# Routing of a mixture of experts in fewer VectorE steps, mixing weights made among the expert blocks, and blocks in another order

## The chip, the cores and the metric

The kernel runs on one core of a Trainium2 chip. Five engines work side by side, each through its own queue in order: TensorE (PE; its weight loads are listed as PEld), VectorE (DVE), ScalarE (ACT), GpSimd (POOL) and SyncE (SP), which issues most transfers. The metric is the device time of one execution in microseconds. A profile of one execution gives the start and the duration of every instruction.

## The reference

A small vision tower: a tokenizer, then layer 0 (attention across images, then six experts of which each row takes two), then layer 1 (a linear attention, then shared and gated MLPs). All is in float32. The part that the change touches is the end of layer 0's attention and its mixture:

```python
h = h + attention(layernorm(h))
x = layernorm(h)
rh = relu(x @ router_w1 + router_b1)
p = softmax(rh @ router_w2 + router_b2)          # 6 experts
top_w, top_i = top_k(p, 2)
weight = softmax(top_w)
out_e = (relu(relu(x @ w1[e] + b1[e]) @ w2[e] + b2[e])) @ w3[e] + b3[e]
h = h + sum of weight * out_e over the two experts chosen
```

There are four images of 784 rows. A row's six logits decide where its normalised row is sent, and its two weights are used only when the experts' results are fetched again for layer 1.

## The kernel before, in words

**Layout.** Rows of an image stand in six tiles of 128 rows with a rest of 16; the four rests share one more tile. A *unit* of routing is what is routed in one go: image 0 (six tiles), image 1 (six), image 2 (six), the first four tiles of image 3, and its last two with the tile of rests (three). So there are five units.

**Attention rounds** (`added_rows` and `weighed`, called for images 1 and 2, and a written-out round for image 3). The order of DVE, PE, ACT and SP is written by hand there. A round for image s does three things in turn on the same engines: the attention of image s (`products`: one DVE pass over 784 columns for each other image, whose sums go to PE as the matmul `pl`; `values`: four more passes a half), the output product of image s-1 with its residual (`attended`), and the routing of image s-2 (`choose`, `count`, `send`).

- `attended` multiplies by `Wo` on PE and adds to `h` on DVE (L965), which also leaves the row sum in `nm`. A tensor_scalar (L969) turns the sums of two or three tiles into minus the mean. ACT then squares `h` minus the mean with a sum (L973).
- `scales_of` takes the root on ACT (L982), `shifts_of` the reciprocal and the product with the mean on DVE (L987, L988). ACT (and for one unit DVE) writes the normalised rows.
- `roots_next` is a dummy Sqrt on one number (`spot`, L922) that makes ACT fetch the Sqrt table before the root needs it.
- `router_logits` makes the logits of a unit on PE in the one buffer of `psum_s`. `choose` (L1058 to L1092) adds the bias on DVE, finds the best and the second expert of every row, and makes running counts of rows per expert over the unit's tiles, starting from `running`. `count` sums the ranks below each row on PE. `send` adds the experts' base addresses `base0` on DVE (L1118), picks each row's place, casts it into `pos` (L1126), and POOL sends the rows to DRAM by indirect DMA (L1129), two for each tile.
- `mix1`, `mix2`, `mix3` turn the two best logits into the two weights `wk`: Exp on ACT, sum, reciprocal and a product on DVE, Exp on ACT, then three DVE steps.

**Where the mixing stands.** For image 0 it is in `weighed(2)`, for image 1 in the written-out round, and for the last three units together behind block 5 of the experts.

**Blocks.** After routing, the rows of an expert lie together in DRAM. They are worked on in 30 blocks: 24 full ones of 256 rows and six small ones of 128, for what is left over. The first seven (`NEARLY`) are full blocks that images 0 and 1 alone fill. They run while the later units are still routed, in a written-out stretch. For block i: SP loads the rows (`load`), PE transposes them (`turned`, `ptb`), ACT copies them out as `xTb`, DVE copies the expert's weights to `own` at an offset which it first loads into a register (`own_weights`, L1487, 1540 columns), PE makes two hidden layers (`hidden`, `pb`, L1511) whose relu goes to ACT (half o = 0) and to DVE or ACT (half o = 1), and `rows_back` makes `pyb` on PE (L1529), adds a bias on DVE (`yb`, L1535) and stores the result through SP.

From block 7 on one loop writes the order: for each i, `load(i + 3)`, `hidden(i, 0)`, `rows_back(i - 1)`, `own_weights(i + 1)`, `turned(i + 1)`, `hidden(i, 1)`. In this loop only DVE, SP and POOL keep the order as written; a scheduler places ACT's and PE's instructions. `order` lists which block comes when: seven early, three full, six small, fourteen full. `after` says behind which block the rows of the first units of layer 1 may be fetched.

Of the kernel before, what the change touches and what calls it, by code (L numbers as in the profile page):

```python
# [29 lines left out]
NI = 4  # L30
# [42 lines left out]
def tile_vit_tower(ctx: ExitStack, tc: tile.TileContext, a: dict, out: bass.AP):  # L73
# [107 lines left out]
    nc.gpsimd.memset(nothing, 0.0)  # L181
    base0 = const.tile([TT, E0], F32, tag="base0", name="base0")
# [768 lines left out]
    def attended(s, two, block=None):  # L951

        if s not in sums:
            sums[s] = [
                small.tile([TT, TPI + 1], F32, tag=tag, name=tag) for tag in ("nm7", "ss7", "r7")
            ]
        nm, ss, r = sums[s]
        pm = mm_rows(
            two, lambda c, j: (
                oL[:, c].rearrange("p b n -> p (b n)") if j == TPI else oTs[s][:, c, cut(j, 1)]  # L960
            ), Wo, "pwo"
        )
        for i, j in enumerate(two):
            ht = h[:, s * TPI + j, :]
            nc.vector.scalar_tensor_tensor(  # L965
                ht, pm[:, i, :], 1.0, ht, ALU.mult, ALU.add, accum_out=nm[:, j : j + 1]
            )
        part = nm[:, two[0] : two[-1] + 1]
        nc.vector.tensor_scalar(part, part, -1.0 / D, None, ALU.mult)  # L969
        if block is not None:  # L970
            turned(block)
        for j in two:
            nc.scalar.activation(  # L973
                junk, h[:, s * TPI + j, :], AF.Square, bias=nm[:, j : j + 1],
                accum_out=ss[:, j : j + 1],
            )


    def scales_of(u):
        b, j0, n = u  # L980
        nm, ss, r = (x[:, j0 : j0 + n] for x in sums[b])
        nc.scalar.activation(r, ss, AF.Sqrt, scale=1.0 / D, bias=eps[:TT])  # L982

    def shifts_of(u):
        b, j0, n = u
        nm, ss, r = (x[:, j0 : j0 + n] for x in sums[b])
        nc.vector.reciprocal(r, r)  # L987
        nc.vector.tensor_tensor(nm, nm, r, ALU.mult)  # L988
# [44 lines left out]
    def router_logits(u):  # L1033
        b, j0, n = u
        rT = turned0.pop(u)
        pr = psum_s.tile([P, 512], F32, tag="pss", name="plg")
        for j in range(n):
            nc.tensor.matmul(
                pr[:TT, j * E0 : (j + 1) * E0], rT[:, cut(j, 1)], rw2, start=True, stop=True
            )  # L1040
        logits0[u] = pr[:TT, : n * E0].rearrange("p (j e) -> p j e", e=E0)
# [3 lines left out]
    def choose(u):  # L1045
# [6 lines left out]

        def wide(x):
            return x.unsqueeze(2).to_broadcast([TT, n, E0])

        rk = rank[E0][:TT].unsqueeze(1).to_broadcast([TT, n, E0])
        lg = t7("lg7", n, E0)
        nc.vector.tensor_tensor(lg, logits0.pop(u), over(rb2, n), ALU.add)  # L1058
        m = t7("m7", n)
        nc.vector.tensor_reduce(m, lg, AX.X, ALU.max)  # L1060
        nc.vector.tensor_tensor(lg, lg, wide(m), ALU.subtract)
# [6 lines left out]
        second = t7("second7", n)  # L1068
# [7 lines left out]
        tiles = t7("tiles7", n + 1, E0)  # L1076
        if running[0] is None:
            nc.vector.memset(tiles[:, 0, :], 0.0)
        else:
            nc.vector.tensor_copy(tiles[:, 0, :], running[0])  # L1080
        nc.vector.tensor_tensor(tiles[:, 1:, :], sel[:, 0], sel[:, 1], ALU.add)
        if n == 6:
            odd = tiles[:, :6].rearrange("p (k i) e -> p k i e", i=2)
            nc.vector.tensor_tensor(odd[:, :, 1], odd[:, :, 1], odd[:, :, 0], ALU.add)
            nc.vector.tensor_tensor(
                tiles[:, 2:4], tiles[:, 2:4], over(tiles[:, 1], 2), ALU.add
            )
            nc.vector.tensor_tensor(tiles[:, 6], tiles[:, 6], tiles[:, 5], ALU.add)
            nc.vector.tensor_tensor(tiles[:, 4:], tiles[:, 4:], over(tiles[:, 3], 3), ALU.add)
        else:  # L1090
            for j in range(n):
                nc.vector.tensor_tensor(tiles[:, j + 1], tiles[:, j + 1], tiles[:, j], ALU.add)  # L1092
        running[0] = tiles[:, n, :]
# [3 lines left out]
    def count(u):  # L1097
# [6 lines left out]
        for k in range(2):  # L1104
# [4 lines left out]
            out_, allones[:TT, :TT], tiles[:, :n, :].rearrange("p j e -> p (j e)"), start=False, stop=True  # L1109
        )  # L1110
        picked[u] = sel, out_.rearrange("p (j e) -> p j e", e=E0)

    def send(u):
# [3 lines left out]
        at = small.tile([TT, n, E0], F32, tag="at7", name="at7")  # L1117
        nc.vector.tensor_tensor(at, before_, over(base0, n), ALU.add)  # L1118
        nc.vector.tensor_tensor(
            sel, sel, at.unsqueeze(1).to_broadcast([TT, 2, n, E0]), ALU.mult  # L1120
# [264 lines left out]
    def weighed(s):  # L1385
# [26 lines left out]
        if s > 1:  # L1412
            mix1(past)
            mix2(past)
# [5 lines left out]
        if s > 1:  # L1420
            mix3(past)
# [28 lines left out]
    order += [(2, i) for i in range(NSMALL)]  # L1450
    order += [(1, i) for i in range(FIRST, NFULL - NEARLY)]
# [124 lines left out]
    with tc.manual_schedule(engines=by_hand | {ENG.SP}):  # L1576
# [3 lines left out]
        mix1(past)  # L1580
# [7 lines left out]
        mix2(past)  # L1588
# [7 lines left out]
        mix3(past)  # L1596
# [73 lines left out]
        for v in (u, ua, ub):  # L1670
            mix1(v)
        hidden(6, 1)
        for v in (u, ua, ub):
            mix2(v)
        for v in (u, ua, ub):
            mix3(v)
# [146 lines left out]
    for u, (b, j0, n) in enumerate(units[:2]):  # L1823
        last = (b * TPI + j0 + n) * TT
        most = {2: 8, 3: 13}[-(-last // BLK)]
        after[u] = order.index((1, most - 1))
    after[LU] = after[2] = NBLK - 1
    assert after[0] < after[1] < NBLK - 1
    with tc.manual_schedule(engines={ENG.DVE, ENG.SP, ENG.Pool}):
        own_weights(NEARLY)  # L1830
        turned(NEARLY)
        for i in range(NEARLY, NBLK + 1):
# [8 lines left out]
            if i == NEARLY + 1:  # L1841
                centred_weights()
            for u in (0, 1, LU, 2):
# [587 lines left out]
```

## Time and profile before

| what | us |
|---|---|
| median of three executions | 735.71 (733.22 to 735.82) |
| the profiled execution's own time | 733.79 |
| its span | 732.1 |
| tokenizer and keys, up to the first round | 0 to about 181 |
| rounds of images 1 and 2 | 181 to 240 |
| last round and wait for the first block | 240 to 263 |
| first seven blocks with routing | 263 to 318 |
| blocks 7 to 29 | 318 to 437 |
| layer 1 | 437 to 732 |

A timeline row has the start, the busy time, engine, line and operation, what is written from what, shapes and a count; in brackets stands how long the engine had been idle before it and who ended that. A row of waits has who waited for whom, then the total, the number of times and the longest. A row by stage has start and end, the length, busy time of PE, PEld, DVE, ACT and POOL (instructions in brackets), the granted TensorE clock, the share of the DMA engines and GB/s.

### The profile page before, as it was taken

The page shows a single profiled execution, that of the slowest core. Times are in us where ns is not written, and L with a number is a line of the kernel's source. Part 1 is how long each engine was busy: PE and PEld are TensorE (multiplying, and loading weights), DVE is VectorE, ACT ScalarE, POOL GpSimd, SP SyncE. Part 2 cuts the span into 40 slices and gives each one's busy share as a digit, 9 for nine tenths or more (in the row PEclk, how much of TensorE's full clock was granted, in tenths as well). Part 3 has the DMA queues.
Part 4 walks back from the last instruction along what each step waited for, and adds up shares of the span by engine and source line. Part 5 has one row for each costly group of instructions (what it writes and reads, how often), then busy time and mean ns, then how long its engine had stood idle before and what let it go on. Part 6 is the DMA issues. An engine that isn't in the chain of part 4 may idle for free.

```text
span 732.1 us, 9866 instructions
## 1 busy us (share of the span) xinstructions
PE 684.2 (93%) x3023; PEld 471.4 (64%) x3023; DVE 480.6 (66%) x1486; ACT 322.7 (44%) x787; POOL 125.0 (17%) x232
## 2 busy tenths in 40 slices
PE   7889988999998879997899998999999999999996
PEld 4636655656566568786788884677776855555553
DVE  5689886778999765455444766779968654354441
ACT  1545546555865663432222326655545232222231
POOL 5400000000034717600003035762000000000000
PEclk9999999999999899999999999999999999999999
DMA  6899999000014754422324352331000014321333
GB/s 181 282 423 418 420 417 414 5 1 1 0 56 138 258 176 157 154 93 67 100 87 130 100 165 76 92 85 40 1 1 1 4 30 119 118 92 54 115 99 102
DMA packets 56477, 96.49 MB, mean 132 GB/s; under 512 B 6697, under 2 KB 46351, under 8 KB 56425
## 3 DMA queue, kind: packets, MB, share of 16 engines
q1 hardware_dynamic: 49924, 79.69, 31.0%
q0 software_dynamic: 5600, 14.32, 6.5%
q10 hardware_dynamic: 900, 1.86, 0.8%
q8 instruction: 24, 0.39, 0.2%
q14 instruction: 29, 0.23, 0.1%
HBM read 30.75 MB, written 65.09 MB: 131 GB/s over the span
## 4 chain that ended last, share of the span: by engine, by line
PE 54%; DVE 6%; ACT 2%; issue 1%; DMA 1%; DVEq 1%; SPq 0%; ACTq 0%
PE pb L1511 12%; PE pe L315 6%; PE pyb L1529 5%; PE ps L315 5%; PE pqk L1972 4%; PE ps L2381 3%; PE pout L2151 3%; PE pout L2156 3%; PE pukx L2071 2%; PE pt L306 2%; PE pe L2351 2%; PE ps L2375 2%; PE ptb L1496 1%; DVE own L1487 1%; PE pkvo L2131 1%
## 5 line engine op out<-in xcount | busy, mean ns | idle before, releaser
L1129 POOL DMA_INDIRECT xrows<-xn,pos x50 | 53.1, 1063 | 220.3 <-DVE nm L988 179.5
L1729 POOL DMA_INDIRECT ys<-yrows,pos x50 | 48.8, 976 | 138.3 <-DMA yrows<-yb 120.6
L1511 PE MATMUL pb<-xTb,own 128*128 128x256 f32 (+1 forms) x240 | 54.4, 371 | 9.3 <-DVE own L1487 8.2
L1517 ACT ACTIVATE hb<-pb,own 128x256 f32<-128x256 f32 (+1 forms) x74 | 33.8, 457 | 56.0 <-PE pb L1511 49.7
L1511 PEld LDWEIGHTS pb<-xTb,own 128*128 128x128 f32 x240 | 41.7, 195 | 17.5 <-ACT hb L1517 6.4
L1511 PE MATMUL pb<-hb,own 128*128 128x256 f32 (+1 forms) x240 | 52.2, 360 | 0.5 <-DVE hb L1519 0.5
L1529 PE MATMUL pyb<-own,hb 128*128 128x256 f32 x216 | 51.8, 381 | 0.2 <-ACT hb L1517 0.2
L315 PE MATMUL pe<-xT,eW 128*128 128x512 f32 (+1 forms) x112 | 46.0, 553 | 0.0
L1972 PE MATMUL pqk<-Wqkv,lxT 128*128 128x512 f32 x100 | 44.9, 594 | 0.2 <-ACT lxT L94 0.2
L1529 PEld LDWEIGHTS pyb<-own,hb 128*128 128x128 f32 x216 | 40.3, 190 | 5.9 <-ACT hb L1517 0.6
L1511 PEld LDWEIGHTS pb<-hb,own 128*128 128x128 f32 x240 | 40.4, 190 | 4.9 <-DVE hb L1519 1.2
L630 PE MATMUL pw<-Wall,pT 128*128 128x512 f32 (+1 forms) x96 | 42.5, 593 | 0.0
L1500 ACT COPY xTb<-ptb 128x512 f32<-128x512 f32 (+1 forms) x30 | 16.3, 543 | 57.7 <-PE ptb L1496 57.7
L1535 DVE TENSOR_TENSOR yb<-pyb,eb 128x512 f32<-128x512 f32 (+1 forms) x30 | 19.1, 638 | 33.9 <-PE pyb L1529 33.5
L1519 DVE TENSOR_SCALAR hb<-pb,own 128x256 f32<-128x256 f32 (+1 forms) x46 | 20.5, 446 | 27.9 <-PE pb L1511 21.2
L890 DVE SCALAR_TENSOR_TENSOR prod<-kq 128x784 f32<-128x784 f32 x32 | 30.4, 969 | 6.2 <-ACT kq L1317 3.4
L306 PEld LDWEIGHTS pt<-ident,xn 128*128 128x128 f32 x200 | 24.4, 145 | 15.5 <-issue 6.3
L315 PEld LDWEIGHTS pe<-xT,eW 128*128 128x128 f32 x112 | 20.2, 190 | 21.6 <-issue 16.5
L1487 DVE COPY own<-kq 128x1540 f32 x30 | 28.8, 963 | 7.8 <-ACT xTb L1500 2.4
L306 PE MATMUL pt<-ident,xn 128*128 128x128 f32 x200 | 29.5, 285 | 3.5 <-ACT xn L1003 1.6
L630 PEld LDWEIGHTS pw<-Wall,pT 128*128 128x128 f32 (+1 forms) x96 | 17.9, 189 | 20.1 <-issue 17.1
L1972 PEld LDWEIGHTS pqk<-Wqkv,lxT 128*128 128x128 f32 x100 | 18.4, 190 | 19.3 <-issue 17.0
(422 smaller groups left out, 1442.0 us busy)
## 6 DMA issues: line engine op xcount, KB each, us to landing
xrows<-nothing SPq DMA_DIRECT2D x22, 896.0 KB
yrows<-nothing SPq DMA_DIRECT2D x22, 896.0 KB
out_dram<-h SPq DMA_DIRECT2D x23, 384.0 KB
xb<-xrows SPq DMA_DIRECT2D x24, 256.0 KB
yrows<-yb SPq DMA_DIRECT2D x24, 256.0 KB
kq<-in_L_ffn_expert_w_dram SPq DMA_DIRECT2D x18, 256.0 KB
wb<-wd SPq DMA_DIRECT2D x16, 128.0 KB
img<-in_x_dram SPq DMA_DIRECT2D x5, 294.0 KB
```

The costliest lines, as they stand in the source:

```text
L306: nc.tensor.transpose(pt[:, j * TT : (j + 1) * TT], xn[:, j, c * P : (c + 1) * P], ident[:TT, :TT])
L315: nc.tensor.matmul(pm[: wcols.stop - wcols.start, :n], w[:, c, wcols], xT(c), start=(c == 0), stop=(c == chunks - 1),)
L630: nc.tensor.matmul(pm, pixels(c, tiles[j]), Wall[: K1[c], c, :], start=(c == 0), stop=(c == 1))
L890: nc.vector.scalar_tensor_tensor(prod, qTs[s][:, o, :], 1.0, kT[:, o, t * SEQ : (t + 1) * SEQ], ALU.mult, ALU.mult, accum_out=atts[s][:, o ...
L1129: put = nc.gpsimd.indirect_dma_start(out=xrows[:, :], out_offset=bass.IndirectOffsetOnAxis(ap=pos[:, k, t0 + j : t0 + j + 1], axis=0), in_ ...
L1487: nc.vector.tensor_copy(w, ewf[0][:, bass.ds(off, EW)])
L1511: nc.tensor.matmul(pm, wm[:, c, o * P : (o + 1) * P], src[:, c, :], start=(c == 0), stop=(c == 1),)
L1517: nc.scalar.activation(dst[:, o, :], pm, AF.Relu, bias=b)
L1529: nc.tensor.matmul(pm[:, t, :], src[:, c, t * P : (t + 1) * P], wm[:, c, :], start=(c == 0), stop=(c == 1),)
L1729: got = nc.gpsimd.indirect_dma_start(out=y[:, j, k, :], out_offset=None, in_=yrows[:, :], in_offset=bass.IndirectOffsetOnAxis(ap=pos[:, k, ...
L1972: nc.tensor.matmul(pqk, xTs[u][:, c, cut(j, 1)], Wqkv[:, c, : 2 * D], start=(c == 0), stop=(c == 1),)
L2151: nc.tensor.matmul(pm[:, i, :], xT[:, c, cut(j, 1)], Wvo[:, c, :], start=(c == 0), stop=False,)
```

## The change

1. The row sums in `nm` stay as sums. The Square takes `scale=-D` with the sum as its bias, the root `scale=1/D**3`, and the product of shift and root is a scalar_tensor_tensor with -1/D. The tensor_scalar L969 is gone (13 instructions).
2. The router's bias is added on PE, by a matmul of one row of ones with `rb2`, ahead of the logits in the same accumulation. `choose` reads the logits from PSUM.
3. The running counts are made by one tensor_tensor_scan along (expert, tile), with a table `onward` that is 0 at each expert's start, instead of four additions (six tiles) or one for each tile (four and three tiles).
4. `base0` is added on PE in `count`, by a fourth matmul; `send` multiplies with the counts straight from PSUM.
5. The mixing of all five units moves into the block loop: `mix1` behind block 10, `mix2` behind block 11, `mix3` behind block 12. The logits and the second value are kept in five buffers each.
6. Behind the first three later full blocks, small and full blocks alternate.

```diff
+    onward = {}
+    for n in (TPI, GT, TPI + 1 - GT):
+        onward[n] = const.tile([TT, E0, n + 1], F32, tag=f"onward{n}", name="onward")
+        nc.gpsimd.memset(onward[n], 1.0)
+        nc.gpsimd.memset(onward[n][:, :, 0], 0.0)
...
-        part = nm[:, two[0] : two[-1] + 1]
-        nc.vector.tensor_scalar(part, part, -1.0 / D, None, ALU.mult)
...
-                junk, h[:, s * TPI + j, :], AF.Square, bias=nm[:, j : j + 1],
+                junk, h[:, s * TPI + j, :], AF.Square, scale=-float(D), bias=nm[:, j : j + 1],
...
-        nc.scalar.activation(r, ss, AF.Sqrt, scale=1.0 / D, bias=eps[:TT])
+        nc.scalar.activation(r, ss, AF.Sqrt, scale=1.0 / D**3, bias=eps[:TT])
...
-        nc.vector.tensor_tensor(nm, nm, r, ALU.mult)
+        nc.vector.scalar_tensor_tensor(nm, nm, -1.0 / D, r, ALU.mult, ALU.mult)
...
+        nc.tensor.matmul(
+            pr[:TT, : n * E0], allones[:1, :TT], over(rb2, n)[:1], start=True, stop=False
+        )
...
-        nc.vector.tensor_tensor(lg, logits0.pop(u), over(rb2, n), ALU.add)
+        logits = logits0.pop(u)
         m = t7("m7", n)
-        nc.vector.tensor_reduce(m, lg, AX.X, ALU.max)
-        nc.vector.tensor_tensor(lg, lg, wide(m), ALU.subtract)
+        nc.vector.tensor_reduce(m, logits, AX.X, ALU.max)
+        nc.vector.tensor_tensor(lg, logits, wide(m), ALU.subtract)
...
-        if n == 6:
-            odd = tiles[:, :6].rearrange("p (k i) e -> p k i e", i=2)
-            nc.vector.tensor_tensor(odd[:, :, 1], odd[:, :, 1], odd[:, :, 0], ALU.add)
...
+        upto = t7("upto7", E0, n + 1)
+        nc.vector.tensor_tensor_scan(
+            upto.rearrange("p e j -> p (e j)"), onward[n].rearrange("p e j -> p (e j)"),
+            tiles.rearrange("p e j -> p (e j)"), 0.0, ALU.mult, ALU.add,
+        )
...
+        nc.tensor.matmul(out_, allones[:1, :TT], over(base0, n)[:1], start=False, stop=True)
...
-        at = small.tile([TT, n, E0], F32, tag="at7", name="at7")
-        nc.vector.tensor_tensor(at, before_, over(base0, n), ALU.add)
...
-        if s > 1:
-            mix1(past)
-            mix2(past)
...
-        if s > 1:
-            mix3(past)
...
-    order += [(2, i) for i in range(NSMALL)]
-    order += [(1, i) for i in range(FIRST, NFULL - NEARLY)]
+    for i in range(NSMALL):
+        order += [(2, i), (1, FIRST + i)]
+    order += [(1, i) for i in range(FIRST + NSMALL, NFULL - NEARLY)]
...
-        for v in (u, ua, ub):
-            mix1(v)
         hidden(6, 1)
-        for v in (u, ua, ub):
-            mix2(v)
-        for v in (u, ua, ub):
-            mix3(v)
...
-        after[u] = order.index((1, most - 1))
+        after[u] = max(order.index((1, most - 1)), order.index((2, NSMALL - 1)))
...
+            for k, mix in enumerate((mix1, mix2, mix3)):
+                if i == NEARLY + 3 + k:
+                    for v in list(mixed):
+                        mix(v)
```

## The prediction

> **What bounds the kernel now.** I read the busy table, then busy time by stage, then the chain of work, the waits, and the timeline around each edit. Times in microseconds from the span's start; the span is 732.1, its execution 733.79, so 1.7 lie outside it.
>
> ```profile
> span 732.1 us, 9866 instructions
> PE 684.2 (93%) x3023; PEld 471.4 (64%) x3023; DVE 480.6 (66%) x1486; ACT 322.7 (44%) x787; POOL 125.0 (17%) x232
> 189.00:214.00 25.00, 23.02 (x99) 15.66 (x99) 22.88 (x69) 17.93 (x41) 1.39 (x2) 1.00 0.00 1
> 240.00:263.00 23.00, 16.11 (x72) 11.78 (x72) 16.72 (x55) 15.85 (x40) 11.45 (x12) 0.85 0.81 264
> 263.00:300.00 37.00, 36.47 (x189) 31.14 (x189) 20.96 (x85) 16.93 (x36) 21.63 (x21) 0.95 0.45 151
> 335.00:360.00 25.00, 19.79 (x137) 17.67 (x136) 11.94 (x24) 6.80 (x18) 0.00 (x0) 1.00 0.29 87
> ```
>
> The last four rows are stages: start:end, length, then busy time of PE, PEld, DVE, ACT, POOL, then clock, DMA share, GB/s. In an attention round (189 to 214) PE and DVE are both nearly full. Before the first block (240 to 263) neither is. From 263 to 300 PE is full. In the run of small blocks (335 to 360) PE idles 5.2.
>
> The timeline says what holds 240 to 263: unit 1's twelve scatters on POOL, the loads on SP that wait for the last, then the first weight copy `own`.
>
> ```profile
> 237.05 0.17 DVE L1126 CAST pos<-place 128x12 int32<-128x12 f32 x1
> ...
> 237.99 0.96 POOL L1129 DMA_INDIRECT xrows<-xn,pos  x1 [8.65 <-ACT junk L973]
> ...
> 255.60 3.94 SPq L1466 DMA_DIRECT2D xb<-xrows  x4
> ...
> 262.17 0.96 DVE L1487 COPY own<-kq 128x1540 f32 x1 [1.59 <-DMA xb<-xrows]
> ```
>
> The first scatter follows the cast of `pos` by 0.77 and the page's releaser (ACT) is only the last event before it; the chain of work runs scatter, loads, `own`, PE. So what moves the cast moves the first block.
>
> **The change, part by part. Attention.** DVE rows give the price of each step taken out. The sum's scaling L969: 0.17, but 0.20 of DVE's time (181.08 to 181.28). `lg` add: 0.22 from start to start. Four adds of the running counts: 0.66. `at`: 0.22. Six mixing steps of a six-tile unit: 0.60 + 0.54.
>
> The scan is in no row. Lower bound: a 36-column TENSOR_TENSOR, 0.20; upper: the 0.66 it replaces. [...] The rows give 0.16 fixed and about 1 ns a column[...]. `choose` gets 0.22 + 0.66 - 0.26 = 0.62 shorter.
>
> *Round of image 1 (181 to 189).* Three L969 off DVE, but the product matmul at 188.94 waits 0.20 for DVE behind PE's own 188.74: gain 0.2.
>
> *Round of image 2.* DVE would save 0.62 + 3 x 0.20 + 0.22 = 1.4. It doesn't keep it. In the loop over blocks ScalarE isn't ordered by hand, so the built program moves the first two Exps of `mix1` up to where their inputs exist: in rounds 2 and 3 they stand between the `spot` activation, which fetches the Sqrt table early, and the six Squares. ScalarE then holds load Sqrt, `spot`, load Exp, Exp, Exp, Squares, load Sqrt, root `r`, load for Tanh: two loads more a round. The first is covered: ACT idles 5.42 before the Squares. The second stands behind the last Square, in front of `r`:
>
> ```profile
> 210.84 0.19 ACT L973 ACTIVATION_READ_ACCUMULATOR junk<-h,nm 128x1 f32 x1
> 211.06 0.30 ACT L982 ACTIVATE r<-ss,eps 128x6 f32<-128x6 f32 x1
> ...
> 211.38 1.28 ACT L879 ACT_TABLE_LOAD   x1
> 211.39 0.19 DVE L987 RECIPROCAL r<-r 128x6 f32<-128x6 f32 x1
> ```
>
> Today DVE's reciprocal starts 0.03 after `r`. Afterwards the Squares begin at 205.7 (the first row sum comes 1.2 earlier), six at 0.64 end at 209.55, the load 1.28 to 210.83, `r` to 211.13, reciprocal 211.15 instead of 211.39. DVE, ready at about 209.8, stands there, with two products behind it and PE's product matmul (213.72) behind those. Net 0.24, round 1's 0.2 in it. [...] Here the load took 1.28 and the Tanh behind it began 0.01 after its end; I take 1.28. [...]
>
> *Round of image 3.* Ahead of the cast at 237.05, DVE loses the mixing of unit 0 (1.14), 0.62 of `choose`, two L969 and the uncovered 0.07 of a third (0.47), `at` (0.22): 2.45, with the 0.24 carried 2.7. PE doesn't stop it: ScalarE's copies of `xT` no longer wait 1.65 for a mixing Exp, so PE's output products start with `oT` about 1.4 earlier and reach the counts in time. The late `r` comes after the cast here, so the table load hurts only products that PE's gate matmuls (busy to 239.02) hold anyway. Scatters, loads and `own` move from 262.17 to 259.5: **-2.7** (ends: -1.3, if the product matmul of image 3, which gains only that, decides instead; -2.7). Unit 1's mixing, 245 to 256, goes from a stretch that waits for the scatters: nothing.
>
> **The first blocks, PE full.** Two matmuls a unit are new, `rb2` and `base0` through `allones`, each in the two passes every f32 matmul shows. Nearest rows: plg, 12 passes in 1.50; pcount, 4 in 0.53; so 0.26 each. Five fall after 263: +1.3. PE's wait of 0.25 for `tiles` (281.39) goes: **+1.05**. The Exp table now comes at about 270.8 in front of `hb1(0)`, which gets 0.8 late; its reader at 275.44 has 2.6 spare. With the mixing gone from 310 to 316, the copy `xTb` at 314.57 needn't stand behind an Exp: 0.37 of PE's 1.05 wait, **-0.4**. POOL's memsets of `onward` end before 12, where POOL idles 7.4.
>
> **The blocks' order.**
>
> ```profile
> PE pb L1511 <- DVE own L1487: 5.8, 7, 1.2
> 347.50 1.03 PE L1529 MATMUL pyb<-own,hb 128*128 128x256 f32 x4
> 348.60 0.42 DVE L1535 TENSOR_TENSOR yb<-pyb,eb 128x256 f32<-128x256 f32 x1 [0.49 <-PE pyb L1529]
> 349.37 0.96 DVE L1487 COPY own<-kq 128x1540 f32 x1 [0.35 <-ACT xTb L1500]
> 350.48 1.13 PE L1511 MATMUL pb<-xTb,own 128*128 128x128 f32 x8 [0.84 <-DVE own L1487]
> ```
>
> `own` starts 0.77 after `yb` whatever `yb`'s size (0.42 or 0.69): its register load fills that. From the start of `pyb` to the next hidden layer it takes 2.98 behind a small block's `pyb`, 3.81 behind a full one's (334.43 to 338.23). PE covers it with `pyb` (0.86 or 1.73), the next turn (0.22 or 0.43) and a hidden layer (0.97 or 1.73). Alternating: small to full 3.81 - 3.13 = 0.68, full to small 2.98 - 2.81 = 0.17. The same sum for small to small gives 0.93 where 0.85 was measured, so 0.08 comes off each: 6 x 0.60 + 5 x 0.09 = 4.0. Now: 0.80 + 1.22 + 0.86 + 0.84 + 0.85 + 0.65 = 5.2. Gain 1.2, or 0.8 if the single 1.22 is chance: **-1.0**. So mixing moves the wait rather than covers it. Same loads and stores on SP, three ahead.
>
> **Mixing weights among the blocks.** Five units now meet in blocks 11 and 12: 15 DVE steps each. The nine of each kind took 1.80 (312.62 to 314.42) and 1.57: 2.9 and 2.55 for fifteen. Queued behind the first fifteen: block 12's `hb0`, `yb(11)`, `own(13)`; on ACT, block 13's `xTb` behind five Exps. From PE's end of hidden(11): `hb0(12)` is ready at 4.0, PE wanted it at 3.2; `own(13)` follows 0.95 late. The second fifteen make block 13's second layer 0.6 late, of which 0.45 reaches block 14. **+1.4**.
>
> **Sum**: -2.7 + 1.05 - 0.4 - 1.0 + 1.4 = -1.65 on 733.79, or 732.1. The three runs (median 735.71) and this execution average 734.6; the forecast for a median is 734.6 - 1.65 = **733.0**. Half a per cent (3.7) is about what a measurement of this kernel can tell from no change.
>
> **Rivals.** *Alternation covers `own`*: 5.2 instead of 1.0: 728.8. For it: PE is full in every full block. Against: 3.13 under 3.81. *Round 2 keeps DVE's 1.4*, if the load before `r` finds cover: 731.8. Against: the reciprocal is 0.03 behind `r` now. *The first block isn't the scatters' to move*: -1.3 there, 734.4. *Slower: half clock at the first block.* PE ran at half clock from 263.3 to 266.7 after idling 2.4, and from 242.8 to 249.7 after the longer gap round 240. Its last work before the first block moves up more than `own` does, so the gap becomes 3.5. [...] It decides from a half-clock stretch of 6.8 on.
>
> **How the numbers follow.** Forecast 0.40, own range 731.3 to 734.7; cover 0.20; round 2 0.12; not the scatters 0.13; half clock 0.15. The range 729.5 to 736.5 leaves out the lower half of the cover case and the far end of half clock. Faster by over 0.5% (below 732.0): 0.18 from cover, 0.07 from round 2, 0.09 from the forecast's low end: 0.34. Slower (above 739.4): 0.05. Same: 0.61.
>
> **What would show it.** A load of 1.28 between the last Square and `r` near 210, DVE waiting about 1.4 for it; first scatter near 235.3; `own` near 259.5; waits for `own` in the mixed blocks summing to about 4, at full blocks; stalls at blocks 12 to 14. Wrong if DVE doesn't wait for `r`, if the waits for `own` vanish, or if half clock there lasts 6.8.

## The result, and the profile after

The changed kernel took 732.56 us (median of 10 runs, 731.47 to 733.94) against 735.45 for the kernel before (10 runs, 732.86 to 735.82): a ratio of 0.9971, 95% interval 0.9958 to 0.9983. On another chip, beside other runs of the kernel before, it was 0.9985 (0.9972 to 0.9997). The forecast was 733.0, within 0.5% of no change, and that is where it came out. The profiled execution has a span of 730.3 against 732.1, 1.8 less, where the sum of the prediction had 1.65 less. The sum is right; two of its five terms are not, and that they cancel, with 0.7 that had no term, is luck.

The page of the changed kernel, its first lines, then busy time by stage (start:end, length, PE, PEld, DVE, ACT, POOL, clock, DMA share, GB/s):

```profile
span 730.3 us, 9886 instructions
PE 688.0 (94%) x3043; PEld 473.0 (65%) x3043; DVE 476.0 (65%) x1449; ACT 327.5 (45%) x791; POOL 126.7 (17%) x238
189.00:214.00 25.00, 23.67 (x102) 16.29 (x101) 21.97 (x63) 21.00 (x45) 3.08 (x3) 1.00 0.03 11
240.00:258.90 18.90, 15.63 (x68) 11.32 (x67) 14.29 (x38) 13.09 (x30) 9.57 (x10) 0.83 0.84 275
258.90:300.00 41.10, 40.62 (x214) 34.27 (x215) 19.40 (x74) 21.21 (x50) 25.43 (x25) 1.00 0.47 162
330.00:360.00 30.00, 26.59 (x149) 23.04 (x150) 17.49 (x54) 8.52 (x23) 0.00 (x0) 1.00 0.27 84
```

VectorE lost 37 instructions and 4.6 us, PE gained 20 instructions and 3.8 us, ScalarE four (the table loads). In the attention round VectorE fell from 22.88 to 21.97 of 25 and ScalarE rose from 17.93 to 21.00. PE still has no slack in the first blocks (40.62 of 41.10); in the small and full blocks of 330 to 360, 3.4 of 30 are idle. The half clock that stood at the first block (a granted clock of 0.50 from 263.2 to 266.5 before, 0.95 over 263 to 300) is gone: 1.00 over 258.9 to 300.

Around the first block the timeline now reads as follows. The cast and the first scatter come 3.05 earlier than before, the loads 2.49, the first `own` 4.42:

```profile
234.00 0.17 DVE L1132 CAST pos<-place 128x12 int32<-128x12 f32 x1
234.94 0.96 POOL L1135 DMA_INDIRECT xrows<-xn,pos  x1 [7.14 <-issue]
253.11 3.94 SPq L1468 DMA_DIRECT2D xb<-xrows  x4
256.74 0.63 PE L1498 MATMUL ptb<-ident,xb 128*128 128x128 f32 x4 [0.47 <-DMA xb<-xrows]
257.75 0.97 DVE L1489 COPY own<-kq 128x1540 f32 x1 [0.67 <-DMA xb<-xrows]
258.86 1.97 PE L1513 MATMUL pb<-xTb,own 128*128 128x256 f32 x8 [0.63 <-DVE own L1489]
```

In round 2 the table load stands where the prediction put it, between the last Square and the root, and VectorE waits for the root:

```profile
208.92 0.19 ACT L976 ACTIVATION_READ_ACCUMULATOR junk<-h,nm 128x1 f32 x1
209.12 1.28 ACT L985 ACT_TABLE_LOAD   x1
210.42 0.30 ACT L985 ACTIVATE r<-ss,eps 128x6 f32<-128x6 f32 x1
210.75 0.19 DVE L990 RECIPROCAL r<-r 128x6 f32<-128x6 f32 x1 [1.32 <-ACT r L985]
```

One place after another shows where the 1.8 was made and lost. `pl` is the gate matmul that ends a round's scores; `pyb(i)` is the start of block i's second-layer product on PE, from PE's timeline.

| place | before | after | gained so far | gained here | predicted here |
|---|---|---|---|---|---|
| `pl`, round 1 | 188.94 | 188.47 | 0.47 | 0.47 | 0.2 |
| `pl`, round 3 | 240.45 | 238.45 | 2.00 | 1.53 | |
| first `own` | 262.17 | 257.75 | 4.42 | 2.42 | 2.7 for all three rows |
| `pyb(0)` | 275.44 | 271.30 | 4.14 | -0.28 | |
| `pyb(5)` | 309.98 | 306.95 | 3.03 | -1.11 | -1.05 for both rows |
| `pyb(6)` | 317.01 | 313.61 | 3.40 | 0.37 | 0.4 |
| `pyb(9)` | 334.43 | 331.03 | 3.40 | 0 | 0 |
| `pyb(22)` | 399.07 | 396.58 | 2.49 | -0.91 | 1.0 - 1.4 = -0.4 |
| `pyb(28)` | 433.44 | 431.30 | 2.14 | -0.35 | 0 |
| end of span | 732.1 | 730.3 | 1.8 | -0.34 | 0 |

So three things ask for experiments: why the first block gained 4.4 and not 2.7; why the mixed order gave nothing in the blocks; and what the moved mixing is worth in all.

### The profile page after: what moved, and what is told of

Its sections match the earlier page's. It is cut to its first block, busy times and chain, and to the rows that moved or that the text cites. A ratio compares the mean times of both kernels' runs of the same rounds, so it can differ in the third digit from the quotient of the medians.

```text
span 730.3 us, 9886 instructions
## 1 busy us (share of the span) xinstructions
PE 688.0 (94%) x3043; PEld 473.0 (65%) x3043; DVE 476.0 (65%) x1449; ACT 327.5 (45%) x791; POOL 126.7 (17%) x238
## 3 DMA queue, kind: packets, MB, share of 16 engines
q10 hardware_dynamic: 900, 1.86, 0.8%
## 4 chain that ended last, share of the span: by engine, by line
PE 53%; DVE 6%; ACT 2%; DMA 2%; issue 2%; DVEq 0%; POOL 0%; ACTq 0%; SPq 0%; POOLq 0%
PE pb L1513 11%; PE pe L320 6%; PE pyb L1531 6%; PE ps L320 5%; PE pqk L1969 3%; PE ps L2378 3%; PE pout L2148 3%; PE pout L2153 3%; PE pukx L2068 2%; PE pt L311 2%; PE pe L2348 2%; PE ps L2372 2%; PE ptb L1498 1%; DVE own L1489 1%; PE pkvo L2128 1%
```

## The experiments

They ran on four chips. On the two that the first eight runs used, the kernel before took 768 to 774 us. In each of those eight traces ScalarE or VectorE stands idle for 7 us or more up to a point between 282 and 307, and in most again, for 8 to 17, up to 477 to 508. TensorE then waits, and the granted clock is low there: in the run with the order alone 0.6 and 0.8 in the page's slices from 290 to 328, 0.8 and 0.7 in those from 483 to 522. In that run, for example:

```profile
294.29 0.47 ACT L1518 ACTIVATE hb<-pb,own 128x256 f32<-128x256 f32 x1 [8.13 <-remote]
507.94 5.28 PE L1973 MATMUL pqk<-Wqkv,lxT 128*128 128x512 f32 x8 [13.84 <-ACT lxT L94]
```

(The copy `lxT` that TensorE waited for had itself waited 15.68, `remote`.) `remote` means that the profile names no instruction that ended the wait; what held ScalarE is open. From those runs I read stages outside such stretches and draw nothing from their totals unless said.

### The order alone

```diff
 (the kernel before)
-    order += [(2, i) for i in range(NSMALL)]
-    order += [(1, i) for i in range(FIRST, NFULL - NEARLY)]
+    for i in range(NSMALL):
+        order += [(2, i), (1, FIRST + i)]
+    order += [(1, i) for i in range(FIRST + NSMALL, NFULL - NEARLY)]
...
-        after[u] = order.index((1, most - 1))
+        after[u] = max(order.index((1, most - 1)), order.index((2, NSMALL - 1)))
```

> The kernel before with the mixed order of the blocks alone. Theory: in a small block PE is bound by a loop (second-layer product pyb, its result yb, the register load, the copy own, the next hidden layer, the next pyb), and each turn of it depends on one pyb and one hidden layer whatever stands beside them; so a small and a full block take 3.95 + 5.62 = 9.57 us in any order. The last pyb of the blocks starts at 433.4 as before (0.15 either way), the time is the same (ratio 1.000, within 0.1%), and the waits for own are still about 5.0 us, at other blocks. The prediction's step: 1.0 less, the last pyb at 432.4.

Measured: `pyb(9)` at 357.24, `pyb(22)` at 421.87, with the granted clock at 0.9 or more in all of the page's slices there: 64.63 us for the thirteen blocks, against 64.64 in the kernel before. Ratio 0.9987 (0.9954 to 1.002), no more than this chip could tell. The waits of that stretch and of the block ahead of it, in the run's list (total, times, longest), against 5.8, 7, 1.2 in the kernel before (the list in the prediction):

```profile
PE pb L1512 <- DVE own L1488: 4.8, 8, 0.9
```

The listed waits fell by the 1.0 that was forecast (within the thirteen blocks alone, from 5.2 to 4.2), and the time did not. The list counts idle time from a modelled end of the matmuls, and so leaves a part of each wait out: a small block behind a full one starts 1.93 behind the hidden layer ahead of it (383.44 to 385.37), where it takes 1.73 without a wait (361.98 to 363.71 in the next run), and this 0.20 is in no list. PE's busy time in the stretch rose from 59.32 to 60.27 for the same work.

The order is worth 0.01. Why, the changed kernel's PE shows in the mixed blocks:

```profile
370.97 1.89 PE L1531 MATMUL pyb<-own,hb 128*128 128x256 f32 x8
374.79 1.97 PE L1513 MATMUL pb<-xTb,own 128*128 128x256 f32 x8 [0.59 <-DVE own L1489]
376.59 1.03 PE L1531 MATMUL pyb<-own,hb 128*128 128x256 f32 x4
379.59 1.13 PE L1513 MATMUL pb<-xTb,own 128*128 128x128 f32 x8
380.55 1.89 PE L1531 MATMUL pyb<-own,hb 128*128 128x256 f32 x8
```

A second-layer product releases `yb`, `yb` stands ahead of the register load and of `own` on VectorE, `own` releases the next hidden layer, and behind that hidden layer stands the next second-layer product. That is a closed loop: 3.82 + 1.80 with a full `pyb` and a full hidden layer, 3.00 + 0.96 with small ones. The hidden layer behind `pyb(i-1)` is that of block i+1, so in alternation a full product is again followed by a full hidden layer and a small one by a small one, as the lines show; the sum of a pair is 9.58. In the run of small blocks before, it was 3.95 a small block and 5.62 a full one, 9.57. Each block brings one leg of each kind, so the sum does not depend on the order. PE's work fills a full block anyway.

### Own ahead of yb

```diff
 (the changed kernel, loop over blocks)
+            own_weights(i + 1)
             rows_back(i - 1)
-            own_weights(i + 1)
```

> The changed kernel with the copy own of block i+1 issued ahead of yb of block i-1 in the loop over blocks (from block 7 on). If the loop through yb and own is what bounds the small blocks, the waits for own fall from 5.1 us to under 1 and the stretch from the second layer of block 9 to that of block 22 becomes 3 to 5 us shorter, the whole about 4 us (0.5%) shorter than the changed kernel. Rival: VectorE is itself full enough there that yb comes late by as much as own comes early (0.6 behind small blocks), and the next wait, for the relu of the hidden layer, takes over: under 1.5 us.

Measured: `pyb(9)` 337.36, `pyb(22)` 397.05: 59.69 us against 65.55, 5.86 less, more than expected. A pair of a small and a full block takes 8.59 (360.90 to 369.49), and PE is busy all of it. On VectorE, `own` now runs while `yb` would still be waiting for `pyb`, and in PE's list of waits for those blocks one wait for `own` is left, at the mixing (the second list line, for a relu, lies ahead of `pyb(9)`):

```profile
374.24 0.96 DVE L1489 COPY own<-kq 128x1540 f32 x1 [0.43 <-issue]
375.12 0.69 DVE L1537 TENSOR_TENSOR yb<-pyb,eb 128x512 f32<-128x512 f32 x1
```

```profile
PE pb L1513 <- DVE own L1489: 0.6, 1, 0.6
PE pb L1513 <- DVE hb L1521: 0.5, 1, 0.5
```

The loop through `yb` and `own` was the cause; the rival (VectorE too full) falls.

### The Exps held

```diff
 (the changed kernel, mix1; for lg and second)
+            put = nc.scalar.activation(x, x, AF.Exp)
+            tc.add_manual_dep(put.ins, held_by[0, 1], ...)   # behind block 0's second hidden layer
```

> The changed kernel with the first two Exps of each unit's mixing held behind block 0's second hidden layer, so that no Exp stands between the Squares in rounds 2 and 3 of attention (4 function table loads fewer before the blocks). VectorE's waits for the root r fall from 1.32 and 1.13 to below 0.4. Theory: the gate matmul pl of round 2 moves from 213.07 to about 212, the cast of round 3 from 234.0 to about 232.7; the first own follows by 1 only if the expert weights it also waits for have landed, otherwise by 0.3. Whole: 0.3 to 1.3 shorter, 1.0 likeliest. Rival: PE bounds the rounds and nothing moves (0).

Measured: VectorE no longer waits for `r` in rounds 2 and 3. `pl` of round 2 came at 212.20 (0.87 earlier), the cast at 233.05 (0.95), `pl` of round 3 at 237.50 (0.95: nothing more, so the second late root cost nothing, as predicted). The loads came 0.94 earlier. The first `own` came 0.12 earlier:

```profile
252.17 3.94 SPq L1474 DMA_DIRECT2D xb<-xrows  x4
256.87 0.08 DVE L970 DVE_READ_ACCUMULATOR h<-pwo,h 128x1 f32 x1
257.63 0.96 DVE L1495 COPY own<-kq 128x1540 f32 x1 [0.67 <-DMA xb<-xrows]
258.74 1.97 PE L1519 MATMUL pb<-xTb,own 128*128 128x256 f32 x8 [1.29 <-DVE own L1495]
```

The cast, the scatters and the loads gained 0.95, and `own` did not follow. It is not the transfer named in the brackets that holds it, but VectorE's attention tail. The register load ahead of `own` is not counted as busy, but `prof` lists it by its source line. In the kernel before:

```profile
260.30 0.08 DVE L965 DVE_READ_ACCUMULATOR h<-pwo,h 128x1 f32 x1
260.42 0.17 DVE L969 TENSOR_SCALAR nm<-nm 128x2 f32<-128x2 f32 x1
L1485 DVEq TENSOR_LOAD <-meta x2: 321/432/544, 260.4 to 263.5; - x2
```

and in the changed kernel:

```profile
256.31 0.42 DVE L970 SCALAR_TENSOR_TENSOR h<-pwo,h 128x256 f32<-128x256 f32 x1 [0.46 <-PE pwo L331]
257.00 0.08 DVE L970 DVE_READ_ACCUMULATOR h<-pwo,h 128x1 f32 x1
L1487 DVEq TENSOR_LOAD <-meta x2: 319/434/549, 256.3 to 258.3; - x2
```

With the scaling of the sums in place, the load starts with the scaling, behind both `h` steps; without it, it starts with the first of the two `h` steps and runs beside them. From that `h` step to `own` it takes 1.44 or 1.45 in all eleven traces of kernels without the scaling, while the time from the first load of `xb` to `own` goes from 3.37 to 9.75 in them. So the loads hold `own` in none of them. With the scaling it is 2.57 (kernel before), 2.58 (order alone) and 2.22 (mixing alone); the first two have a stop of 0.36 among the copy's semaphore waits, of which more at the end.

Nor is the tail of a fixed length. `own` came 20.13 behind `pl` of round 3 here, 19.30 in the changed kernel, and 20.03 in the run with own ahead of yb, whose code is the same up to there. Of this 0.83, `pr` on PE took 0.34 (3.72 instead of 3.38; in the changed kernel the granted clock over it was 0.80, and in the kernel before, where it took 3.94, 0.68), and VectorE waited 0.54 for a `pwo` that the changed kernel does not wait for (why is not shown). So what the tail had gained with `pl` was lost in it. (I had expected the expert weights to hold `own`; the semaphore waits ahead of the copy pass one after another, in the changed kernel four of about 50 ns from 257.4 to 257.7, so they don't.) The gain came back behind it: `pyb(0)` was 0.79 earlier, since ScalarE's copies were further on and PE's 0.48 for `xT` was gone. 0.8 in all, 1.0 expected.

### The scatters later

```diff
 (the changed kernel, send, for unit 1, ahead of the scatters)
+            for _ in range(3):
+                filler = nc.gpsimd.tensor_copy(late, pos[:, 0, t0 : t0 + 1].to_broadcast([TT, 512]))
```

> The changed kernel with three copies on POOL (each 128 x 512, of the positions just made, read by nobody) between the cast of unit 1's positions and its first scatter; they hold the scatters and the loads behind them by D, about 1.5 to 3 us. The prediction's step (what moves the cast moves the first block): the first own D later. Theory: own stands behind VectorE's attention tail and not behind the scatters, so it stays within 0.3 of its place counted from the gate matmul pl of round 3 (19.3 us after it in the changed kernel, 19.9 to 20.1 in its variants); the first hidden layer then waits for the turned rows xTb instead, and comes D - 1.1 to D - 0.5 later.

Measured, beside a run of the changed kernel on the same chip (there `pl` of round 3 at 238.49, own at 257.81, first hidden layer at 258.92; here `pl` at 239.41, since an early half-clock stretch was longer in this run and cost 0.9: the granted clock was 0.62 in 100 to 104 and 0.53 in 104 to 108, there 0.88 and 0.69):

```profile
235.21 1.96 POOL L1137 COPY late<-pos 128x512 int32<-128x512 int32 x3 [6.43 <-DVE pos L1132]
237.32 1.60 POOL L1142 DMA_INDIRECT xrows<-xn,pos  x1 [0.15 <-issue]
255.56 3.94 SPq L1481 DMA_DIRECT2D xb<-xrows  x4
258.93 0.96 DVE L1502 COPY own<-kq 128x1540 f32 x1 [0.67 <-DMA xb<-xrows]
259.20 0.63 PE L1511 MATMUL ptb<-ident,xb 128*128 128x128 f32 x4 [1.75 <-DMA xb<-xrows]
260.53 1.97 PE L1526 MATMUL pb<-xTb,own 128*128 128x256 f32 x8
```

The scatters are 1.42 later behind the cast. From `pl` to `own` it takes 19.52 (19.32 without): 0.2 later, which is what PE's half clock took (`pr` 3.60 against 3.40, the granted clock 0.54 against 0.70 in 244 to 248). From `pl` to the first hidden layer 21.12 (20.43): 0.69 later, now behind the turned rows, for which PE waits 1.75 instead of 0.47 in the first profile. It is one execution. So in the changed kernel the first block has two chains that end within a microsecond of each other, and the longer one is VectorE's attention tail.

### The mixing back at its old places, three times

```diff
 (the changed kernel: calls put back)
+            mix1(past); mix2(past)   # attention rounds, as before; mix3(past) at their end
+        for v in (u, ua, ub): mix1(v) # block 6, then mix2 and mix3
-                if i == NEARLY + 3 + k: ...
```

> The changed kernel with the mixing weights made where they were made before (units 0 and 1 inside rounds of attention, the rest at block 6); routing steps and order as changed. Theory: VectorE gets 1.14 more in round 3 and 0.6 to 0.75 more in the tail after it, but loses the waits for r (about 1.0 of each): the first own 0.9 to 1.5 later than in the changed kernel (258.6 to 259.3); the wait for xTb at block 7 comes back (+0.4); the stalls at blocks 12 to 14 go (-1.3). Sum 0 to +0.6 on the changed kernel. The prediction's steps: -1.4 + 0.4 in the blocks and about +1 before them, so 0. Rival: the mixing is what moved the first block, 3 us of it: +2.

> The kernel with the mixing at its old places once more, since in the first run of it ScalarE stood 2.3 us at a copy of xT for nothing that the profile shows, ahead of the first block. Without that stand: first own at 258.5 to 259.5 (257.75 in the changed kernel), second layer of block 9 to that of block 22 in 63.9 us against 65.55. Net 0 to -0.8 on the changed kernel. Rival: the stand is part of this order of ScalarE's work and comes again: first own at 261 or later.

> The kernel with the mixing at its old places (routing steps and order as changed), for a reading without the extra half-clock stretches of the chip of the first two runs of it. Theory from those: gate matmul of round 1 to that of round 3 in 51.1 us (50.0 in the changed kernel), from there to the first own 20.2 to 20.9 (19.3), so the first own at about 260.5; second layer of block 6 another 0.4 later for the wait for xTb; second layer of block 9 to that of block 22 in 63.9 to 64.3 (65.55). Sum: 1 to 2 us longer than the changed kernel, level with the kernel before. Prediction's steps: 0 to +1. Rival: the 2.3 us stand of ScalarE at the copies of xT comes back: first own at 262.5 or later, 3 to 4 longer.

The first run had `pl` of round 1 to that of round 3 in 51.13 us (in the changed kernel 49.98), but ahead of its first `own` (263.18) ScalarE stood 2.29 at a copy of `xT`, for nothing that the profile shows. In the second run a half-clock stretch lay in round 3 and everything came later (mean granted clock of the execution 0.975, of the first run's 0.981); counted from `pl` of round 3 its first `own` (263.36) took 20.87, where the first run's took 23.21, so the stand of 2.29 did not come again. The third, on a chip without the further stretches, has neither: back-to-back copies, and one half-clock stretch of 3.4 at 224 (granted clock 0.85 in 220 to 224, 0.73 in 224 to 228; the eight matmuls of `pr` take 4.26 there and 2.85 in the repeat of the changed kernel). I put it at 1.7 of PE's time, an estimate, half of 3.4; the first run, without it, has 51.13, 1.62 less. With that taken out:

| | mixing back | changed | moved mixing gains |
|---|---|---|---|
| `pl` round 1 to `pl` round 3 | 52.75 - 1.7 = 51.05 | 49.98 | 1.07 |
| to the first `own` | 20.55 | 19.32 | 1.23 |
| first hidden layer to `pyb(0)` | 11.78 | 12.62 | -0.84 |
| `pyb(5)` to `pyb(6)` | 7.03 | 6.66 | 0.37 |
| `pyb(9)` to `pyb(22)` | 63.92 | 65.57 | -1.65 |

(The changed kernel's values are those of its repeat, told below.) Together 0.2 up to `pyb(22)`: the moved mixing gives up to 2.3 at the first `own` and takes it back behind it. The second and third row are not the mixing's alone. In this run PE's half clock ends later behind `pl` (granted clock 0.50 in 244 to 248 and 0.74 in 248 to 252, with `pl` at 240.72; in the repeat 0.70 and 1.00, with `pl` at 238.49), and `pr` takes 4.13 where it takes 3.40 in the repeat of the changed kernel: 0.73 of the 1.23. The other 0.5 are `mix3`'s three steps on VectorE (255.62 to 256.13):

```profile
247.31 4.13 PE L320 MATMUL pr<-xT,rw 128*128 128x512 f32 x8
255.62 0.17 DVE L1283 TENSOR_SCALAR z<-second 128x6 f32<-128x6 f32 x1
256.13 1.57 DVE L941 SCALAR_TENSOR_TENSOR oT<-vT,att,oT 128x272 f32<-128x272 f32 x3
```

`mix2`'s steps cost nothing: VectorE waits 1.83 for PE behind them. And the run with own ahead of yb, with the mixing moved, also takes 11.78 to `pyb(0)`: where `own` comes later, the waits behind it go. Of the 1.65 in the blocks, 1.29 are the stalls: `pyb(11)` to `pyb(12)` took 6.53 where the same pair of forms takes 5.61, and the next 4.34 where it takes 3.97. Another 0.36 is a late register load, of which more at the end. The kernel as a whole was 734.33 against 734.43, ratio 0.9998 (0.9987 to 1.0008): level with the kernel before, as was expected. Of the first `own`'s gain of 4.4, then, about 1.6 was the mixing's (1.07 and 0.5).

### The mixing alone

The kernel before with the same move of the mixing (the converse of the diff above).

> The kernel before with the mixing moved among the blocks and nothing else. The first two Exps of each unit float into rounds 2 and 3 again, so the root's table load returns: VectorE's reciprocal in round 2 at about 212.6 where it was 211.39, pl of round 2 up to 1.0 later. The cast of round 3 is then level (-1.1 for the mixing, +1.0 for the wait), the tail after it 0.6 to 0.75 shorter: first hidden layer 0.5 to 1.5 earlier than 263.28. Blocks 11 to 14: 1.3 longer; xTb at block 7: 0.4 shorter. Net -0.6 to +0.5. Rival (mixing was most of the first block's 4.4 us): 3 earlier at the first hidden layer, net -2.

Measured: ratio 1.0027 (1.0005 to 1.0049), slower if anything. VectorE's waits for `r` were 1.25 and 2.01. The wait for `xTb` at block 7 went (`pyb(5)` to `pyb(6)` 6.66 instead of 7.03). `pyb(9)` to `pyb(22)` took 66.50 against 64.64, 1.86 more, where 1.3 was expected. In fact the bunched mixing cost more in the small blocks: two of them took 5.34 and 5.17 where 3.96 is usual, 2.6 together, and the two late register loads that the kernel before has in this stretch (0.36 each) were not there. A half-clock stretch in round 2 and another at 244 to 252 (mean granted clock of the execution 0.960) spoil the reading of the first block. Nor does the total decide on the rival: TensorE's mean clock was 0.964 in these runs and 0.966 in those of the kernel before beside them, about as much apart as the ratio shows. Against 3 us for the mixing speak the runs with it put back (1.6, at most 2.3).

### The biases back on VectorE

```diff
 (the changed kernel)
-        nc.tensor.matmul(pr[...], allones[:1, :TT], over(rb2, n)[:1], start=True, stop=False)
+        nc.vector.tensor_tensor(lg, logits0.pop(u), over(rb2, n), ALU.add)
-        nc.tensor.matmul(out_, allones[:1, :TT], over(base0, n)[:1], start=False, stop=True)
+        nc.vector.tensor_tensor(at, before_, over(base0, n), ALU.add)
```

> The changed kernel with rb2 and base0 added on VectorE as before (two steps of 0.22 a unit), so without the five pairs of bias matmuls after the first block. The prediction put such a pair at 0.26 us of PE; the trace of the changed kernel reads 0.33 to 0.37 from start to start. Theory: from the first hidden layer to the second layer of block 5 it takes 1.3 to 1.7 us less, and the first hidden layer comes 0 to 0.4 later for VectorE's four steps in rounds 2 and 3. Net 1.0 to 1.4 shorter than the changed kernel. Rival: with the adds back on VectorE, PE waits for it at the counts (0.25 each as before), and the net is under 0.5.

Measured: from the first hidden layer to `pyb(1)`, with three of the five pairs in it, 18.47 against 19.80 in the run with own ahead of yb, whose code is the same up to there but for the biases: 1.33 less, 0.44 a pair. Rounds 1 to 3 were not longer (49.84 against 49.98). Behind 284 lies a half-clock stretch (mean granted clock of the execution 0.975, in the changed kernel's repeat 0.990), so the other two pairs can't be read here; the last experiment has them. The pairs' price, in the changed kernel, from start to start:

```profile
265.01 0.40 PE L1114 MATMUL pcount<-upto,allones 128*128 128x36 f32 x2
265.34 0.41 PE L1118 MATMUL pcount<-base,allones 1*128 1x36 f32 x2
265.67 1.99 PE L1513 MATMUL pb<-hb,own 128*128 128x256 f32 x8
```

The pair for `base` takes 0.33, though it contracts over one row only, as much as the pair ahead of it over 128; and that pair ahead takes 0.33 where it took 0.22 (270.13 to 270.35 before). Together 0.44. It is not that the pair ahead now reads the scan's result: in this run it still does, with no pair behind it, and takes 0.22 (264.86 to 265.08). In front of the first hidden layer of block 1 the pair for `rb2` takes 0.33 and the eight matmuls behind it 0.91 instead of 0.81.

### All of it

```diff
 (the changed kernel with own ahead of yb and the Exps held)
-                if i == NEARLY + 3 + k:
-                    for v in list(mixed):
-                        mix(v)
+                j = i - (NEARLY + 3) - k
+                if 0 <= j < len(mix_order):
+                    mix(mix_order[j])
```

> The changed kernel with own copied ahead of yb, the Exps held, and the mixing spread one unit to a block (each step of a unit one block behind the step before it, blocks 10 to 16). Theory: first second-layer product 0.8 earlier than in the changed kernel (as with the Exps held alone); second layer of block 9 to that of block 22 in 58.2 to 58.7 us, against 65.55 changed and 59.69 with own ahead alone; the whole about 8 us (1.1%) shorter than the changed kernel. Rival: with own ahead, VectorE is full enough that the spread mixing costs as much as the bunched one: 59.7 us there, 6.7 shorter in all.

> The kernel with own ahead of yb, Exps held and mixing spread, and with the two biases back on VectorE. Theory: all gains add: from the first hidden layer to the second layer of block 1 in about 18.0 to 18.5 us (20.3 in e8_all's trace, 18.5 with the biases on VectorE alone), second layer of block 9 to that of block 22 in 58.2 us, the whole about 1.4 us shorter than e8_all and 9.5 (1.3%) shorter than the changed kernel. Rival: with the other waits gone VectorE has no room before the first block and the four adds there cost what PE gains: level with e8_all.

Measured: `pyb(9)` to `pyb(22)` in 58.22 and 58.23, as expected, so the spread mixing costs nothing in the blocks. With the biases on VectorE too (second text), on a chip without further half-clock stretches (mean granted clock 0.990 to 0.992): 720.74 us (4 runs, 720.34 to 722.41) against 735.56, ratio 0.9812 (0.9786 to 0.9837); the changed kernel beside it had 733.70. That version beats both by 13 to 15 us.

```profile
span 720.6 us, 9851 instructions
PE 683.2 (95%) x3023; PEld 471.9 (65%) x3023; DVE 476.1 (66%) x1459; ACT 322.4 (45%) x787; POOL 127.1 (18%) x238
257.11 0.63 PE L1502 MATMUL ptb<-ident,xb 128*128 128x128 f32 x4 [1.78 <-DMA xb<-xrows]
```

`pyb(0)` to `pyb(5)` took 34.27 against 35.63: 1.36 for three pairs, 0.45 each. A miss: the first hidden layer to `pyb(1)` took 19.93 where 18.0 to 18.5 was expected. The last line shows why the first hidden layer came no earlier: `pl` of round 3 and with it VectorE's tail came 1.5 earlier than in the changed kernel beside it, the loads only 0.2, and PE waits 1.78 for the rows that the scatters bring. Here the prediction's chain holds at last. Behind it PE waits again for ScalarE's `xn` and `xT`, as in the changed kernel; in the run with the biases alone, with a later `own`, it did not.

### The changed kernel again

The same kernel, on the last-named chip.

> The changed kernel itself, on the chip of these experiments, beside the kernel before. If what the variants of the changed kernel showed on this chip (2% and more under the kernel before, where half as many microseconds ran at half clock) comes with the change, its ratio here is 0.975 to 0.985; if only the stages count, 0.997. The stages: first own 69.3 us after the gate matmul of round 1, second layer of block 9 to that of block 22 in 65.5 us.

Measured: 733.70 (12 runs), ratio 0.9985 (0.9972 to 0.9997): the stages alone, not 0.98. Its marks repeat the first profile to 0.02: the first `own` 69.30 after `pl` of round 1, and 65.57 for `pyb(9)` to `pyb(22)`.

## Why the prediction was right in sum, point by point

**Step 1, before the first block: -2.7; measured -4.4.** Its pieces were near: scan 0.24 for 42 columns (0.25 taken, an estimate, since no row showed a scan), cast 3.05 earlier (2.7), first scatter at 234.94 (235.3), VectorE's wait for `r` 1.32 (1.4), and the second late root free, as said. The switch of tables cost no more than its load: 1.28, and `r` began 0.02 behind its end. The step that failed is the sentence "what moves the cast moves the first block". Holding the Exps moved the scatters and left `own`; delaying the scatters by 1.4 moved `own` by 0.2, the clock's. `own` waited for VectorE's tail, in the kernel before too: the bracket there (1.59, `xb<-xrows`) is a register load that starts behind the scaling, and the run with the order alone has the same 1.60 with another name in it (`bqkv`). Place by place, the 4.42 are 0.47 in round 1, where 0.2 was taken; 1.53 in rounds 2 and 3, 1.07 of it the mixing's; and 2.42 behind `pl` of round 3. These last are 0.56 of PE at half clock (`pr` 3.38 against 3.94, the granted clock over it 0.80 against 0.68), 0.74 of VectorE's time (`mix3` about 0.5, the rest the scalings), and 1.12 at the register load: 0.76 since it no longer stands behind a scaling, 0.36 since it is not late. I had put down unit 1's mixing in that stretch as "from a stretch that waits for the scatters: nothing", and had not asked what the scaling that was taken out held up behind it. The share of the clock is luck: `pr` took 3.38, 3.40 and 3.55 in three runs of the same code up to there.

**Step 2, first blocks: +1.05; measured +1.39.** A pair costs 0.44, not 0.26: about 2.2 for five. The 0.25 for `tiles` went, as said. The term left out is the clock: the half-clock stretch at the first block went (granted clock 0.52 before and 1.00 after from the first hidden layer to the next `pt`), 1.59 of PE's time from the first hidden layer to the next `pt`, and 0.85 of it came back at once as waits for ScalarE's `xn` and `xT` (0.22 and 0.63, the same steps in both timelines). 2.2 - 0.25 - 1.59 + 0.85 is 1.2.

**Step 3, xTb at block 7: -0.4; measured -0.37.** Alone too (the mixing alone: 0.37).

**Step 4, order: -1.0; measured 0.** The failing step is "0.08 comes off each". The uncorrected sum gave 6 x 0.68 + 5 x 0.17 = 4.9 for the mixed order against 5.2 with a late register load of 0.37 in it: no gain. A correction seen on one kind of wait was then taken off eleven others, and it went the wrong way: the list shows 0.84 for a wait where 348.58 to 350.48 is 1.90 and the same eight matmuls take 0.89 without one (366.77 to 367.66 with own ahead), so 1.01 was lost. The sign named for this step, listed waits of about 4, came true (4.2) without any gain. The loop says why.

**Step 5, mixing in blocks 11 and 12: +1.4; measured +1.29**, in the two places named.

**The rivals.** That alternation covers `own` falls with the order alone. That round 2 keeps its 1.4 falls with the 1.32 wait. That the first block isn't the scatters' to move was right in what it denied and wrong in its number, since it looked for what else could hold the block only in PE. The slower one, more half clock, went the other way: `own` came so much earlier that PE idled 0.63 there and not 3.5. (In the kernel before, a granted clock of 0.50 followed an idle time of 2.41. How long a stretch follows which idle time was not shown; that a gap of 3.5 would bring more of it was my estimate.)

What the sum had no term for: 0.35 between `pyb(22)` and `pyb(28)`, a late register load that stood elsewhere before, and 0.34 in layer 1, where PE waits 0.2 for `xaL` and 0.3 more for `acc`. Without these two the result would have been 0.7 further from the forecast.

## What to carry to other kernels

Where two engines hand work to and fro, write down the loop and add its legs before reordering the jobs in it: legs that belong to each job keep their sum in any order (here 9.58 against 9.57), and only taking a leg out of the loop (here, the copy issued ahead of the step that waits: 8.59) shortens it. Before believing a releaser named in brackets, look for a register load among the rows of the copy's source lines, and compare runs: here the time from the `h` step to the copy stayed at 1.44 or 1.45 while the time from the first load to the copy went from 3.37 to 9.75, so the loads held nothing. A small step that has to wait for the one ahead of it can also hold up a register load behind it: taking it out gave 0.17 of work and 0.76 of waiting. A list of waits that rests on modelled ends can fall with no time saved (here by 1.0, for 0.01); measure from start to start. Where two chains end within a microsecond of each other, shortening one gives no more than that distance (here VectorE's tail 1.5 earlier brought the first hidden layer 0.48 earlier).

## What the runs showed that I had not expected

The register load ahead of `own` came 0.36 late at fixed places of a program: twice in the kernel before (`own` at 341.45 and 384.92, 1.13 behind the start of `yb` where 0.77 is usual), twice in the changed one, at the same two places in its repeat, and nowhere between `pyb(9)` and `pyb(28)` with the mixing back. The same 0.36 lies ahead of the first `own` in the kernel before and in the run with the order alone, between the third and the fourth of the copy's semaphore waits, and not in the other runs. Nothing in the views says what is fetched or waited for; I leave it open.

The same kernel (mixing back) had ratios of 0.9998 (0.9987 to 1.0008), 0.9876 (0.9809 to 0.9943) and 0.9833 (0.9774 to 0.9891) on three chips. On the latter two the mean granted clock of TensorE was 0.976 in it, and 0.966 and 0.964 in two relatives of the kernel before (the order alone, the mixing alone). The stages are the same on all three (`pyb(9)` to `pyb(22)` in 63.92, 63.92 and 63.91); the difference lies in the stretches where ScalarE or VectorE stood, and in the low clock there. Why the variants of the changed kernel stood less on those chips is not known. On an undisturbed chip the half clock shows in small: a stretch at 100 to 108 that was longer in one run (the scatters later, granted clock 0.62 and 0.53 in its halves) than in another (the changed kernel beside it, 0.88 and 0.69) moved everything behind it by 0.9 (`pl` of round 1 from 188.51 to 189.40).
